# The values' bias inside the shared block product, a new order of a graph's operations, and the first weights on another DMA queue: a two-layer graph network on one Trainium2 core

## The chip, the cores and the metric

The kernel runs on one core of a Trainium2 chip. The metric is the device time of one launch, in microseconds. Engines are named as in the profile: PE is TensorE's matmul stream, PEld its weight loads, DVE is VectorE, ACT is ScalarE, POOL is GpSimd, SP is SyncE, which here only issues DMAs. A name with q, as SPq, is the engine's instruction queue.

## The reference

64 graphs of 256 nodes with 256 features go through two layers, all in float32. Cut to what matters:

```python
# layer 0, for each of 64 graphs: x (256, 256), adj (256, 256)
q = heads(x @ Wq + bq); k = heads(x @ Wk + bk)          # 8 heads of 32
attn = softmax(q @ k.T / sqrt(32))
for r in range(4):                                       # four relations
    v_r = heads(x @ Wv[r] + bv[r])
    out += (attn * (adj == r)) @ v_r
x = ln(x + out @ Wo + bo)
x = ln(x + gelu(x @ W1 + b1) @ W2 + b2)
# layer 1
h = gat(gat(x, adj, W1, a1), adj, W2, a2)                # masked softmax over nodes
h = ln(x + h)
x = ln(h + relu(h @ w_ff1 + b_ff1) @ w_ff2 + b_ff2)
```

## The kernel before, in words

A graph is one object, and its work is cut into 225 named operations, each a handful of instructions on one engine. The table PLACES gives each name a place on an axis. Graph g's operation stands at g * PERIOD + place, with PERIOD = 60, and all operations of all 64 graphs are sorted by that number and emitted in that order (`manual_schedule`, at the end of the kernel). So the places are no times: they set the order in which each engine meets its instructions, and how graphs are interleaved. An engine works its instructions strictly in that order and waits where an input isn't ready. Weight DMAs (L139, `issue_load`) and the one-time weight preparations (`v_weights`, `gat_weights`, two `ffn_weights`) stand in the same order at places of their own (LOAD_PLACE and LOAD_STEP, V_PLACE, FFA_PLACE, GAT_PLACE, FFB_PLACE). DMAs are issued on SP's queue.

The names, in the order in which a graph passes them (m is a half of the features, with four heads h each):

- load, cast, jT, mask0 to mask4: x and adj come in (L178, L180), adj is cast (L457), transposed by DMA (L462), and compared with 0 to 3 on GpSimd (L479); mask4 is the GAT mask (L471). xT and xS transpose x and form differences of its blocks (L446, L453).
- qk, qkc, s: query and key products (L487), copies out of PSUM on ScalarE (L496, L498), scores of four heads (L537), each with 32 rows of the array.
- max, exp, rec, nrm, eT, eW, eR: softmax on VectorE and ScalarE (L542 to L560), then a transpose through 32x32 squares on VectorE (L306) and a round trip through DRAM (L311 write, L315 read).
- ec copies the transposed weights to PSUM (L568), pm multiplies them with three relations' masks on VectorE (L572), pl with the fourth's on GpSimd (L577), po sums over relations and nodes (L589), each head in 32 columns of the array; oT copies it (L595).
- vp1 to vp7, vc1, va, vb: the values of all relations, by seven block products instead of eight (L511). vc1 copies the first product into block (0, 0) of v (L523, ScalarE), and the va operations (L520, VectorE) build the other blocks by adding products to blocks made before. vb1 and vb0 add the bias (L528, GpSimd).
- y, yb, wo, ya: residual and output product (L609, L613); st, rt, nb, ln: norms 1 to 4 (L347 to L364).
- aT, aW, aR, au, ax, aS, ad, ae: the first feed-forward part. Transposed input, up (L387), Gelu (L395), differences (L410), seven block products down (L422), sums (L430). The same letters with b: the second one, with Relu.
- hT to zdB, h10, h11, h2: the two GAT attentions (L619 to L682); store (L685).

PSUM has eight banks: four for the scores (s0 to s3), one po for the feed-forward sums, one pe for ec, and two, with the tag mm, that nearly all other products share. A product that takes one of the two waits until the last reader of the tile that lay there before is done. Of free banks, a product takes the one that was freed first in program order.

The two halves of the bias as before: block (m, jc) holds features of half m for node block jc, and the chain of the sums is

```python
for n, to, src, i in (("1", (0, 0), (0, 0), 2), ("6", (0, 1), (0, 0), 6), ("7", (1, 0), (0, 1), 7),
                      ("5", (1, 1), (1, 0), 5), ("4", (1, 0), (1, 0), 4), ("9", (0, 1), (0, 1), 5),
                      ("3", (0, 1), (0, 1), 3)):
    ops[f"va{n}"] = lambda to=to, src=src, i=i: self.v_sum(to, src, i)
```

Of the kernel before, what the change touches and what calls it, by code (L numbers as in the profile page):

```python
# [14 lines left out]
ALU = mybir.AluOpType  # L15
AX = mybir.AxisListType

P = 128
# [7 lines left out]

PERIOD = 60.0
PLACES = {
    "load": 51.115, "cast": 61.829, "xT": 85.66, "jT": 95.244, "mask0": 96.779, "qk0": 96.964,
    "qkc0": 97.949, "s0": 114.109, "mask1": 114.874, "max02": 120.516, "max01": 124.15, "exp02": 124.943,  # L30
    "rec02": 126.88, "nrm02": 128.516, "max00": 137.875, "max03": 138.248, "exp01": 142.049, "xS": 142.083,
    "eT02": 142.989, "exp00": 144.909, "rec01": 145.054, "qk1": 145.647, "exp03": 145.994, "eW02": 148.03,
    "rec00": 148.295, "qkc1": 149.435, "rec03": 149.477, "nrm01": 152.334, "mask2": 153.228, "vp1": 153.403,
    "nrm00": 154.4, "eT00": 155.05, "vc1": 155.594, "s1": 155.923, "nrm03": 158.066, "max10": 158.616,
    "max11": 159.127, "vp6": 159.308, "y": 159.875, "eR02": 161.643, "max13": 162.676, "mask3": 162.803,
    "exp10": 163.51, "exp13": 164.265, "va6": 164.378, "eW00": 164.574, "vp7": 165.766, "max12": 166.896,
    "vp2": 167.32, "eT03": 167.321, "exp12": 167.329, "va7": 168.263, "va1": 168.656, "pl02": 168.829,
    "eT01": 170.084, "vp5": 171.47, "vb1": 171.744, "va9": 173.956, "exp11": 174.017, "va5": 174.086,
    "eW01": 174.237, "vp4": 174.322, "rec11": 174.688, "rec10": 175.037, "ec02": 175.434, "nrm10": 175.847,
    "va4": 177.865, "nrm11": 178.881, "eW03": 179.53, "eT11": 180.637, "rec12": 181.004, "eR01": 181.498,  # L40
    "rec13": 182.146, "pm02": 182.221, "vp3": 182.341, "nrm13": 182.509, "eR00": 182.73, "mask4": 182.957,
    "ec01": 183.686, "va3": 183.974, "pl00": 184.596, "pm01": 184.674, "nrm12": 185.397, "eT13": 185.431,
    "eR03": 186.516, "ec00": 187.545, "eW11": 189.732, "eW13": 192.489, "pm00": 192.506, "eR11": 192.805,
    "pl03": 192.932, "pl01": 194.193, "ec03": 194.796, "vb0": 194.872, "pm03": 195.848, "eT10": 196.442,
    "eR13": 197.184, "eT12": 197.655, "po0": 199.032, "ec11": 199.429, "eW10": 200.338, "oT0": 203.052,
    "eW12": 203.488, "eR10": 203.542, "pm11": 203.833, "ec13": 205.99, "pm13": 207.559, "pl11": 208.544,
    "ec10": 209.569, "pm10": 210.783, "eR12": 211.055, "pl13": 211.531, "pl10": 212.738, "yb": 213.806,
    "ec12": 214.966, "pm12": 215.614, "pl12": 216.323, "po1": 224.021, "oT1": 226.193, "wo": 231.792,
    "ya": 235.114, "st1": 235.515, "rt1": 236.411, "nb1": 237.487, "ln1": 240.106, "aT": 241.237,
    "aW": 243.237, "aR": 244.635, "au0": 248.422, "au1": 248.889, "ax0": 249.225, "ax1": 250.028,  # L50
    "au2": 253.377, "aS1": 255.511, "ax2": 257.28, "au3": 257.297, "ag": 259.726, "ax3": 259.931,
    "ar": 263.256, "aS3": 265.084, "aS2": 265.188, "aS4": 266.76, "ad1": 267.736, "ad7": 268.061,
    "ad2": 269.978, "ad3": 270.34, "ad4": 270.945, "ae": 271.281, "ad5": 273.751, "ae1": 274.652,
    "ae7": 275.033, "ad6": 277.637, "ae5": 279.375, "ae6": 281.724, "st2": 283.997, "rt2": 284.29,
    "nb2": 285.905, "ln2": 291.498, "lg2": 293.887, "lb2": 294.79, "hT": 297.683, "hW": 300.513,
    "hR": 303.071, "ga0": 304.63, "gac0": 305.433, "ga1": 305.656, "gac1": 307.317, "ipA": 307.666,
    "zA": 307.902, "zmA": 307.921, "zxA": 308.379, "zeA": 312.657, "zdA": 315.675, "h10": 324.462,
    "h11": 325.343, "h1c0": 325.47, "h1c1": 325.478, "ipB": 327.18, "zB": 327.348, "zmB": 328.529,
    "zxB": 330.271, "zeB": 332.506, "zdB": 332.513, "h2": 335.643, "h2a": 335.996, "st3": 338.835,
    "rt3": 339.209, "nb3": 342.44, "ln3": 344.153, "bT": 344.795, "bW": 353.039, "bR": 353.733,  # L60
    "bu0": 358.326, "bu1": 358.559, "bx0": 358.988, "bu2": 361.425, "bx1": 361.898, "bx2": 361.904,
    "bu3": 362.148, "bx3": 363.223, "bS1": 363.277, "bd1": 364.353, "bg": 366.001, "bS2": 366.044,
    "br": 366.414, "bd5": 366.625, "bS4": 368.189, "bd6": 369.237, "bd2": 371.158, "bd3": 371.454,
    "be1": 372.63, "be5": 372.632, "bd4": 372.862, "bS3": 372.912, "be6": 374.175, "be": 375.364,
    "bd7": 377.598, "be7": 378.628, "st4": 383.514, "rt4": 389.43, "nb4": 404.438, "ln4": 418.122,
    "lg4": 419.704, "lb4": 422.082, "store": 423.961,
}
LOAD_PLACE, LOAD_STEP = 96.0, 3.0
V_PLACE, FFA_PLACE, GAT_PLACE, FFB_PLACE = 100.0, 240.0, 290.0, 300.0

# [11 lines left out]
def kernel(  # L84
# [12 lines left out]
    nc = tc.nc  # L97
    B, N, D = x.shape
    R = Wv.shape[0]
# [5 lines left out]
    C = N // P  # L105
# [28 lines left out]

    loads = []

    def issue_load():
        t, src = loads.pop(0)
        nc.sync.dma_start(t, src)  # L139

    def weight(w, name, mixed=False):

        k, n = w.shape[0] // P, w.shape[1]
        t = const.tile([P, k, n], F32, name=name)
        if mixed:
            mixed_rows(t, w)
        else:
            loads.append((t, w.rearrange("(k p) n -> p k n", p=P)))
        return t
# [13 lines left out]
    def rowvec(v, n, name):  # L163
        t = const.tile([P, n], F32, name=name)
        loads.append((t, _row(v, n)))
        return t
# [21 lines left out]
    bv_r = const.tile([P, KD, R, P], F32, name="bv_r")  # L188
# [4 lines left out]
        loads.append((bv_r[:, m],  # L193
                      bass.AP(tensor=bv.tensor, offset=bv.offset + m * P, ap=[[0, P], [D, R], [1, P]])))
    while loads:
        issue_load()
    wv_t = const.tile([P, 3, R * P], F32, name="wv_t")
    wv_s = {}
    scale = 1.0 / math.sqrt(DH)
# [4 lines left out]
    wo, bo_r = weight(Wo, "wo"), rowvec(bo, D, "bo_r")  # L204
# [44 lines left out]
    def seven_weights(b, t):  # L249


        nc.vector.tensor_tensor(t[0], b[0][1], b[1][1], ALU.add)
        nc.vector.tensor_tensor(t[1], t[0], b[0][0], ALU.subtract)
        nc.vector.tensor_tensor(t[2], b[1][0], t[1], ALU.subtract)
        nc.vector.tensor_tensor(b[0][1], b[0][0], b[0][1], ALU.subtract)
        return {1: b[0][0], 2: b[1][0], 3: t[2], 4: b[1][1], 5: t[0], 6: t[1], 7: b[0][1]}

    def v_weights():
        wv_s.update(seven_weights([[wv[:, k, m].rearrange("p r n -> p (r n)") for m in range(KD)] for k in range(KD)],
                                  [wv_t[:, i] for i in range(3)]))  # L260

# [170 lines left out]
    class Graph:  # L432
# [87 lines left out]
            nc.vector.tensor_tensor(self.v_part(*to), self.v_part(*src), self.ps["v", i], ALU.add)  # L520

        def v_first(self):
            nc.scalar.copy(self.v_part(0, 0), self.ps["v", 1])  # L523

        def v_bias(self, m, jcs):
            v = self.v[m][:, jcs]
            row = bv_r[:, m].rearrange("p r n -> p (r n)")[:, None, :]
            nc.gpsimd.tensor_tensor(v.rearrange("p c r n -> p c (r n)"), v.rearrange("p c r n -> p c (r n)"),  # L528
                                    row.to_broadcast([P, len(range(C)[jcs]), R * P]), ALU.add)

        def scores(self, m):

# [154 lines left out]
        def operations(self):  # L687

            g, ops = self.g, {}
# [8 lines left out]
            for i in range(1, 8):  # L698
                ops[f"vp{i}"] = lambda i=i: self.v_product(i)

            ops["vc1"] = self.v_first
            for n, to, src, i in (("1", (0, 0), (0, 0), 2), ("6", (0, 1), (0, 0), 6), ("7", (1, 0), (0, 1), 7),
                                  ("5", (1, 1), (1, 0), 5), ("4", (1, 0), (1, 0), 4), ("9", (0, 1), (0, 1), 5),
                                  ("3", (0, 1), (0, 1), 3)):
                ops[f"va{n}"] = lambda to=to, src=src, i=i: self.v_sum(to, src, i)
            ops["vb1"] = lambda: self.v_bias(1, slice(0, 1))
            ops["vb0"] = lambda: self.v_bias(0, slice(0, C))
            for r in range(R + 1):
                ops[f"mask{r}"] = lambda r=r: self.mask(r)
            for m in range(KD):  # L710
# [56 lines left out]


    plan = [(LOAD_PLACE + i * LOAD_STEP, len(PLACES), issue_load) for i in range(len(loads))]
    for place, f in (  # L770
            (V_PLACE, v_weights),
            (GAT_PLACE, gat_weights),
            (FFA_PLACE, lambda: ffn_weights(w1, b1_c, g1_c, be1_c, b2_r, be1_r, "ffa", w2, w2_t)),
            (FFB_PLACE, lambda: ffn_weights(f1, bf1_c, gl1_c, bl1_c, bf2_r, bl1_r, "ffb", f2, f2_t))):
        plan.append((place, len(PLACES), f))
    for g in range(B):
        ops = Graph(g).operations()
# [34 lines left out]
```

## Time and profile before

| what | us |
|---|---|
| median of three runs | 3575.66 (3571.31 to 3575.95) |
| the profiled execution, its own time | 3572.94 |
| its span, first to last instruction | 3571.2 |

The granted TensorE clock over the span is 0.985. The page of the profile gives each engine's busy time and share of the span. The chain of waits follows the instruction that ended last back to what released it, and back again, to the start. A timeline line is a run of equal instructions: start, length, engine, line, operation, output and inputs, shape, count, and in brackets the idle time before it with its releaser. A group's line gives busy time and the mean ns of one, then the engine's idle time before it.

### The profile page before, as it was taken

What the parts mean: (1) busy time and instruction counts of PE and PEld (TensorE: products, weight loads), DVE (VectorE), ACT (ScalarE), POOL (GpSimd) and SP (SyncE); (2) the same over time, 40 slices, a digit from 0 to 9 for tenths busy, and PEclk for the clock granted to TensorE, in tenths of its full rate; (3) what the DMA queues carried; (4) which work ended last, traced back from release to release, by engine and by line L of the source; (5) the groups of instructions that cost most, each with busy time, mean ns of one, the idle gap of its engine ahead of it and who ended that gap; (6) DMA issues with size and microseconds to landing.
All of it is one profiled execution on the core that took longest, in us unless ns stands there. A gap on an engine that the chain in (4) does not pass through costs nothing.

```text
span 3571.2 us, 73514 instructions
## 1 busy us (share of the span) xinstructions
PE 3477.1 (97%) x25816; PEld 2704.2 (76%) x25816; DVE 2805.2 (79%) x4952; ACT 2776.8 (78%) x7107; POOL 3117.9 (87%) x3398
## 2 busy tenths in 40 slices
PE   6899999999999999999999999999999999999995
PEld 3677877877877877877877877877877877877875
DVE  5788888888888888788788888888788788788762
ACT  4677877877877877877877877877877877877863
POOL 4688988988988988988988988988988988988974
PEclk8899999999999999999999999999999999999997
DMA  7344444444444444444444444444444444444420
GB/s 198 112 126 127 131 135 127 131 135 127 131 135 127 131 135 128 131 135 126 132 135 125 133 135 125 133 135 122 135 136 122 135 136 122 135 136 123 132 86 27
DMA packets 809890, 457.97 MB, mean 128 GB/s; under 512 B 334256, under 2 KB 718896, under 8 KB 809520
## 3 DMA queue, kind: packets, MB, share of 16 engines
q1 hardware_dynamic: 809520, 453.27, 43.2%
q8 instruction: 203, 3.33, 0.4%
q14 instruction: 167, 1.37, 0.1%
HBM read 243.42 MB, written 201.33 MB: 125 GB/s over the span
## 4 chain that ended last, share of the span: by engine, by line
PE 95%; DMA 1%; DVE 1%; SPq 1%; POOL 1%; ACT 0%; issue 0%; POOLq 0%; ACTq 0%; DVEq 0%
PE po L589 13%; PE ffa_ps L387 12%; PE ffb_ps L387 12%; PE v_ps L511 11%; PE qk_ps L487 6%; PE ffa_po L422 6%; PE ffb_po L422 6%; PE ffa_pq L422 5%; PE ffb_pq L422 5%; PE s L537 4%; PE h_ps L664 3%; PE h_ps L678 3%; PE ga_wps L619 3%; PE wo_ps L609 3%; SPq L139 1%; PE ga_ips L631 0%
## 5 line engine op out<-in xcount | busy, mean ns | idle before, releaser
L572 DVE TENSOR_TENSOR pm<-rel,pe 128x1536 f32<-128x1536 uint8 x512 | 890.9, 1740 | 131.9 <-ACT pe L568 85.3
L577 POOL TENSOR_TENSOR pl<-rell,eT 128x512 f32<-128x512 bf16 x512 | 592.1, 1168 | 29.0 <-DMA eT<-eT_d 24.2
L550 ACT ACTIVATE e<-s,nmax 128x256 f32<-128x256 f32 x1024 | 474.7, 471 | 73.2 <-DVE eT_sq L306 63.6
L387 PE MATMUL ffb_ps<-ffb_T,f 128*128 128x256 f32 x2048 | 458.4, 382 | 24.0 <-DMA ffb_T<-ffb_T_d 23.8
L387 PE MATMUL ffa_ps<-ffa_T,w 128*128 128x256 f32 x2048 | 465.9, 381 | 8.3 <-DMA ffa_T<-ffa_T_d 8.2
L387 PEld LDWEIGHTS ffb_ps<-ffb_T,f 128*128 128x128 f32 x2048 | 392.6, 192 | 106.1 <-issue 39.4
L560 ACT ACTIVATE e<-e,rden 128x256 f32<-128x256 f32 x1024 | 462.4, 506 | 10.3 <-DVE rden L555 10.1
L479 POOL TENSOR_SCALAR rel<-adT 128x512 uint8<-128x512 bf16 x192 | 288.6, 1503 | 198.1 <-DVE pm L572 181.1
L387 PEld LDWEIGHTS ffa_ps<-ffa_T,w 128*128 128x128 f32 x2048 | 381.3, 191 | 57.8 <-ACT e L560 9.6
L520 DVE TENSOR_TENSOR v<-v,v_ps 128x512 f32<-128x512 f32 x448 | 296.0, 672 | 148.2 <-PE v_ps L511 142.5
L589 PE MATMUL po<-pm,v 128*32 128x256 f32 x6144 | 361.6, 384 | 15.7 <-POOL v L528 12.3
L306 DVE STREAM_TRANSPOSE eT_sq<-e 128x512 f32<-128x512 f32 x512 | 350.6, 694 | 3.3 <-ACT e L560 1.9
L395 ACT ACTIVATE ffb_h<-ffb_ps,bf_c 128x256 f32<-128x256 f32 x512 | 214.6, 470 | 160.6 <-PE ffb_ps L387 154.7
L542 DVE TENSOR_REDUCE nmax<-s 128x2 f32<-128x512 f32 x512 | 337.0, 669 | 0.0
L589 PEld LDWEIGHTS po<-pm,v 128*32 128x32 f32 x6144 | 188.7, 110 | 184.1 <-ACT e L560 46.2
L568 ACT COPY pe<-eT 128x512 f32<-128x512 f32 x512 | 303.3, 592 | 17.8 <-DMA eT<-eT_d 12.7
L528 POOL TENSOR_TENSOR v<-v,bv_r 128x512 f32<-128x512 f32 (+1 forms) x128 | 232.9, 1819 | 5.4 <-DVE v L520 1.1
L395 ACT ACTIVATE ffa_h<-ffa_ps,b_c 128x256 f32<-128x256 f32 x512 | 208.5, 475 | 5.5 <-PE ffa_ps L387 3.8
L496 ACT ACTIVATE qT<-qk_ps,bqs_c 128x256 f32<-128x256 f32 x128 | 60.7, 474 | 188.5 <-PE qk_ps L487 188.5
L550 ACT ACTIVATION_READ_ACCUMULATOR e<-s,nmax 128x1 f32 x1024 | 205.8, 201 | 0.0
L354 POOL TENSOR_TENSOR rs_x<-rs_x,nhalf 128x2 f32<-128x2 f32 x256 | 184.0, 719 | 21.3
L430 DVE TENSOR_TENSOR ffa_res<-ffa_po,ffa_res 128x256 f32<-128x256 f32 (+2 forms) x256 | 133.4, 521 | 69.9 <-PE ffa_po L422 65.6
(154 smaller groups left out, 8535.9 us busy)
## 6 DMA issues: line engine op xcount, KB each, us to landing
eT_d<-eT_sq SPq DMA_DIRECT2D x512, 256.0 KB, 2.1
eT<-eT_d SPq DMA_DIRECT2D x512, 256.0 KB, 3.2
xin<-in_x_dram SPq DMA_DIRECT2D x256, 64.0 KB, 2.5
adi<-in_adj_dram SPq DMA_DIRECT2D x64, 256.0 KB, 3.2
y<-in_x_dram SPq DMA_DIRECT2D x64, 256.0 KB, 3.1
ffa_T_d<-ffa_T_sq SPq DMA_DIRECT2D x64, 256.0 KB, 2.6
ffa_T<-ffa_T_d SPq DMA_DIRECT2D x64, 256.0 KB, 2.9
hT_d<-hT_sq SPq DMA_DIRECT2D x64, 256.0 KB, 2.1
```

The source lines that it names most:

```text
L306: nc.vector.transpose(self.sq.rearrange("p a c k y -> p (c k) a y"), src.rearrange("p c (k a x) -> p (c k) a x", k=KD, a=A))
L387: nc.tensor.matmul(p[:, f - f0, :], self.wa[:, k, f * P:(f + 1) * P], self.x.nodes(k), start=(k == 0), stop=(k == KD - 1))
L395: nc.scalar.activation(self.h[half][:, f1 + f, :], self.ps[f0][:, f, :], self.func, bias=self.ba[:, f0 + f:f0 + f + 1])
L422: nc.tensor.matmul(self.p[bank][:, k], a[:, f], seven[self.name[:3]][i][:, f], start=(f == 0), stop=(f == KF // 2 - 1))
L511: nc.tensor.matmul(self.ps["v", i], a, wv_s[i], start=True, stop=True)
L542: nc.vector.tensor_reduce(self.nmax[m, h], self.s4[m][h].rearrange("p (c n) -> p c n", c=C), AX.X, ALU.max, negate=True)
L550: nc.scalar.activation(e[:, ic, :], self.s4[m][h][:, ic * N:(ic + 1) * N], AF.Exp, bias=self.nmax[m, h][:, ic:ic + 1], accum_out=self.den[ ...
L560: nc.scalar.activation(e[:, ic, :], e[:, ic, :], AF.Copy, scale=self.rden[m, h][:, ic:ic + 1])
L568: nc.scalar.copy(self.pe[m, h], self.et[m, h].t.rearrange("p b c k y -> p (b c k y)"))
L572: nc.vector.tensor_tensor(self.pm[m, h], self.rel.rearrange("p r b c k y -> p r (b c k y)"), bc(self.pe[m, h], [P, R - 1, C * N]), ALU.mult)
L577: nc.gpsimd.tensor_tensor(self.pm_l[m, h], self.rel_l.rearrange("p b c k y -> p (b c k y)"), self.et[m, h].t.rearrange("p b c k y -> p (b ...
L589: nc.tensor.matmul(po[hp, :], self.v[m][:, jc, r, hp], w, start=(r == 0 and jc == 0), stop=(r == R - 1 and jc == C - 1))
```

## The change

There are five edits.

1. The bias of half 0 is added where the first product leaves PSUM: vc1 becomes an add on VectorE instead of a copy on ScalarE. Since every other block is built from block (0, 0), the bias of half 0 reaches them all.
2. `v_weights` once replaces the bias row of half 1 by its difference to that of half 0, and vb1 adds that difference to block (1, 0) after va7, from which block (1, 1) is built. It stays on GpSimd with 512 columns. vb0, an add of 1024 columns, is left out.
3. All places are new. load stands at 98.4 instead of 51.1 and store at 490.8 instead of 424.0; the distances between stages, and so the neighbours on each engine, differ throughout. Taken by the remainder after division by 60, TensorE now has s1 directly before po0 (37.6 and 38.3), vp7, vp2, qk1, vp5, s0, vp3, wo in a row, all four of bu, and au0 to au3 near each other.
4. The places of the weight DMAs and preparations are new: LOAD_PLACE from 96 to 164.4, V_PLACE from 100 to 170, FFA_PLACE from 240 to 322, GAT_PLACE from 290 to 376, FFB_PLACE from 300 to 380.
5. The first ten weight DMAs (wq, wk, their biases, the values' weights and biases), which are issued before any planned operation, go to ScalarE's DMA queue; all later ones stay on SP's.

```diff
-LOAD_PLACE, LOAD_STEP = 96.0, 3.0
-V_PLACE, FFA_PLACE, GAT_PLACE, FFB_PLACE = 100.0, 240.0, 290.0, 300.0
+LOAD_PLACE, LOAD_STEP = 164.4, 3.0
+V_PLACE, FFA_PLACE, GAT_PLACE, FFB_PLACE = 170.0, 322.0, 376.0, 380.0
...
-    def issue_load():
+    def issue_load(engine=nc.sync):
         t, src = loads.pop(0)
-        nc.sync.dma_start(t, src)
+        engine.dma_start(t, src)
...
     while loads:
-        issue_load()
+        issue_load(nc.scalar)
...
+    def bias_row(m):
+        return bv_r[:, m].rearrange("p r n -> p (r n)")
+
     def v_weights():
+        nc.vector.tensor_tensor(bias_row(1), bias_row(1), bias_row(0), ALU.subtract)
         wv_s.update(seven_weights([[wv[:, k, m].rearrange("p r n -> p (r n)") for m in range(KD)] for k in range(KD)],
...
         def v_first(self):
-            nc.scalar.copy(self.v_part(0, 0), self.ps["v", 1])
-
-        def v_bias(self, m, jcs):
-            v = self.v[m][:, jcs]
-            row = bv_r[:, m].rearrange("p r n -> p (r n)")[:, None, :]
-            nc.gpsimd.tensor_tensor(v.rearrange("p c r n -> p c (r n)"), v.rearrange("p c r n -> p c (r n)"),
-                                    row.to_broadcast([P, len(range(C)[jcs]), R * P]), ALU.add)
+            nc.vector.tensor_tensor(self.v_part(0, 0), self.ps["v", 1], bias_row(0), ALU.add)
+
+        def v_bias(self):
+
+            nc.gpsimd.tensor_tensor(self.v_part(1, 0), self.v_part(1, 0), bias_row(1), ALU.add)
...
-            ops["vb1"] = lambda: self.v_bias(1, slice(0, 1))
-            ops["vb0"] = lambda: self.v_bias(0, slice(0, C))
+            ops["vb1"] = self.v_bias
```

The new order on TensorE over one period (the remainders of the places after division by 60, so neighbours belong to different graphs):

```
vp7 1.4  vp2 3.6  qk1 5.3  vp5 6.6  s0 8.7  vp3 9.0  wo 9.2
bu0 14.4 to bu3 16.6  vp4 18.1  bd1 20.5  ga0 20.6  ga1 22.1  bd5 23.7  ipA 24.1
bd2 24.8  bd6 25.0  bd3 27.1  bd4 28.0  au0 29.0  bd7 30.2  au1 31.4  au2 32.2  au3 34.8
s1 37.6  po0 38.3  h10 39.9  h11 41.6  vp1 42.6  ad1 42.8  ipB 43.2  ad6 43.5  qk0 44.6
ad7 45.6  vp6 46.7  ad5 50.3  ad2 50.7  h2 52.8  ad3 55.5  ad4 57.8  po1 59.1
```

## The prediction

> **What bounds the kernel now.** I read the page first, then the busy time by stretches, the chain of waits, TensorE's timeline of one graph, and the groups by shape.
>
> ```profile
> span 3571.2 us, 73514 instructions
> PE 3477.1 (97%) x25816; PEld 2704.2 (76%) x25816; DVE 2805.2 (79%) x4952; ACT 2776.8 (78%) x7107; POOL 3117.9 (87%) x3398
> ```
>
> The stretches (columns: stretch, its length, busy us and instructions of PE, PEld, DVE, ACT, POOL, then granted clock, DMA share, GB/s) say where TensorE is not full:
>
> ```profile
> 0.00:50.00 50.00, 26.20 (x86) 13.87 (x86) 21.37 (x41) 19.32 (x59) 17.81 (x23) 0.80 0.76 197
> 50.00:100.00 50.00, 33.35 (x246) 21.47 (x247) 38.00 (x56) 29.58 (x77) 29.42 (x29) 0.76 0.67 188
> 100.00:150.00 50.00, 45.22 (x332) 31.73 (x330) 35.88 (x61) 25.82 (x66) 32.93 (x35) 0.86 0.36 95
> 150.00:200.00 50.00, 45.52 (x319) 32.96 (x320) 38.28 (x66) 37.72 (x99) 34.55 (x39) 0.90 0.38 117
> 200.00:3400.00 3200.00, 3199.70 (x24006) 2499.45 (x24005) 2599.66 (x4585) 2586.27 (x6630) 2903.76 (x3156) 1.00 0.44 131
> 3400.00:3572.00 172.00, 127.11 (x833) 104.69 (x831) 72.01 (x146) 78.06 (x179) 99.44 (x119) 0.88 0.19 56
> ```
>
> From 200 to 3400 us TensorE is never idle and at full clock; the filling of the pipeline (0 to 200) leaves it idle for 50 us, the emptying (from 3400) for 45. The chain of waits gives the beat of the middle:
>
> ```profile
> 1001.33 6.91 PE ffb_ps L387 x32
> 1054.89 6.91 PE ffb_ps L387 x32
> ```
>
> One graph takes 53.56 us, some 61 times in all outside filling and emptying. Busy is not packed, though. In TensorE's timeline (start, length, ..., count), group starts show what a group really costs:
>
> ```profile
> 1023.17 1.05 PE L422 MATMUL ffb_po<-f,ffb_h 128*128 128x128 f32 x8
> 1024.16 2.80 PE L589 MATMUL po<-pm,v 128*32 128x256 f32 x48
> ...
> 1027.75 2.01 PE L664 MATMUL h_ps<-ga_wh,ga_z 128*128 128x258 f32 x8
> 1029.59 1.11 PE L487 MATMUL qk_ps<-xT,wq 128*128 128x256 f32 x4
> ...
> 1039.66 1.15 PE L537 MATMUL s<-kT,qT 32*128 32x256 f32 x16
> 1040.74 1.13 PE L487 MATMUL qk_ps<-xT,wq 128*128 128x256 f32 x4
> 1041.71 1.03 PE L487 MATMUL qk_ps<-xT,wk 128*128 128x256 f32 x4
> 1042.57 0.61 PE L422 MATMUL ffa_po<-w_t,ffa_t 128*128 128x128 f32 x4
> ```
>
> A full-array group of four 256-column matmuls takes 0.86 us (1041.71 to 1042.57). The one right after s takes 0.97, and s itself 1.08 where four rounds of 0.216 are 0.86. So a visit to the tiled forms (32*128 for s, 128*32 for po) costs: about 0.10 at entry (ffb_po 0.99 before po, 0.89 elsewhere), 0.13 to 0.22 at the exit, 0.10 in the first full group after it; 0.41 for s, 0.33 for po. There are four visits a graph.
>
> **What the Trainium skill says.** "TensorEngine Tiling (Array Packing)", Tiling Modes, Key Properties: changing the tiling mode drains the TensorE. The trace agrees (the 0.33 to 0.41 us above). "Trainium Kernel Development and Optimization", Key Constraints: DMAs of the SP and ACT queues run on the same 16 engines; another issuer saves only the sequencer's issue time. In the trace the engines are 0.76 busy in the first 50 us, so there is little spare rate. "ScalarE: Activation LUTs", What ACT_TABLE_LOAD costs: about 1283 ns plus a drain of about 1380. The trace agrees on 1283; the activation follows 10 to 20 ns later (1014.52 + 1.28, next start 1015.82), so I price a load at 1.28.
>
> **The change, part by part.**
>
> *Bias.* Removed per graph: GpSimd's vb0 and ScalarE's copy. Kept: a GpSimd add of 512 columns. Added: one VectorE add that replaces the copy, 672 ns by its row v<-v,v_ps.
>
> ```profile
> L528 POOL TENSOR_TENSOR v<-v,bv_r 128x1024 f32<-128x1024 f32 x64 | 151.4, 2366 | 0.0
> L520 DVE TENSOR_TENSOR v<-v,v_ps 128x512 f32<-128x512 f32 x448 | 296.0, 672 | 148.2 <-PE v_ps L511 142.5 <-POOL v L528 5.7
> L523 ACT COPY v<-v_ps 128x512 f32<-128x512 f32 x64 | 36.9, 577 | 0.0
> ```
>
> Per graph GpSimd falls by 2.37 us from 48.7 (3117.9/64), ScalarE by 0.58 from 43.4, VectorE rises by 0.67 from 43.8 to 44.5. All stay under TensorE's 53.56, so in the middle this alone is worth 0; the cover is TensorE's own work. The new wait: vc1 stands on VectorE between pm13 and pm11; behind it are pm11 and zmB (which the second GAT attention waits for), and TensorE's qk0 waits for the PSUM buffer that vc1 frees. From vp1's start to qk0 TensorE has 0.86 + 0.89 + 0.22 + 0.89 = 2.86 us (vp1, ad1, ipB, ad6); the product is complete about 1.02 after its start (second matmul at 0.43, 0.59 long), vc1 ends at 1.69. Spare: 1.2 us.
>
> *Places, in the middle.* I put TensorE's new order in a row with the durations above and walked the PSUM and buffer waits. New is that s1 stands directly before po0: three visits instead of four. The switch between the two tiled forms is not in the trace. Cheapest it costs nothing (0.41 saved), dearest as much as two separate visits (0). I take a drain like the others: 0.10 entry, 0.22 for the switch, 0.23 exit against 0.74 now: about -0.2. The 0.09 of the present qk1 after h10 (1029.59 to 1030.54 is 0.95) goes; vp5's wait of up to 0.19 for va7 passes to qk1, which now stands there. The other ties have 0.2 us or more to spare by ScalarE's starts: ipA after gac1, au2 after ax0, h10 after zdA, vp3 after qkc1. Together I take -0.25 us a graph, times 61 = -15 us; bounds -0.5 and +0.3, -30 to +18.
>
> ScalarE loses work too: ax0 to ax3 stand together with no exponential between, so two table loads a graph instead of four (by the groups of shapes now 127 at L395, 65 at L651, 62 at L550): -2.6 us a graph, off the path, but cover for those ties.
>
> *Filling.* The lines of the chain at the start:
>
> ```profile
> 4.20 0.47 SPq L139
> ...
> 54.69 2.31 POOL v L528
> 57.05 5.49 PE po L589 x64
> ...
> 90.37 2.02 DMA ffa_T_d<-ffa_T_sq
> 92.41 2.69 DMA ffa_T<-ffa_T_d
> 95.23 8.55 PE ffa_ps L387 x32
> ```
>
> SP's queue is the chain for most of the first 48 us. Ten weight DMAs leave it (4.20 to 10.0, 5.8 us); ScalarE issues them while idle (its first work is at 9.08), and if they lasted past that, qkc0 would pay. Bandwidth is shared, so xin may land up to 1 us later and the weights 1 to 2 us earlier. Given back: the next graph's four xin and one adi, 3.3 us, now stand before jT and another set before the first eR, and SP waits for the first transpose, some 3 us. Net on the first eR -1. The difference of the two bias rows is one more VectorE op at the head, +0.7, and waits for the last weight DMA. vb0 goes: 2.3 us straight off the chain before po. So po comes about 3 us earlier. Then aT now precedes the FFN weights' subtractions on VectorE (0.7 us each, four of them), whose time overlaps the 4.7 us of DMA: -3. Around the GAT weights (125 to 151 us) hT now comes before them: -4, bounds +6 and -12. Sum -10, bounds -20 and +6.
>
> *Emptying.* It is three rounds of ffb_ps, 40 to 44 us apart, each held by mask, softmax, norm and a DMA round trip. The lags of the stages behind wo differ by under 3 places (ffa 20 after 17, ffb 125 after 127, in places), so 0, bounds ±6.
>
> **Sum.** -15 - 10 = -25 us on the profiled 3572.9 us (span 3571.2 and 1.7 around it). The median of the runs is 3575.7, 2.7 higher; the same -25 gives 3550.
>
> **The rivals.**
> Both savings at their good ends (switch free, fill -20, so -30 - 20 = -50): 3525. For it speaks that all engines but TensorE get lighter on balance; against, that TensorE's order has many near ties. Chance 0.08.
> Nothing arrives: TensorE's 53.56 stays, the switch costs as much as the visit it saves, the weights are bandwidth bound and the fill gives back 5: 3571, range 3568.5 to 3583. Chance 0.13.
> Slower: VectorE serves vc1 late. If pm13 (1.74 us) starts later than 2.86 - 0.67 - 1.74 = 0.45 us after vp1's start, because its ec13 or eR13 is late, TensorE stands at qk0 in every graph; 1 us past that point is 61 us: 3550 + 61 = 3611, range 3583 to 3640. For it: the trace shows pm waiting for pe (85.3 us in 72 waits). Against: two fewer table loads make ec13 early. Chance 0.21.
>
> **The numbers.** Forecast, 3550 (own range 3530 to 3568): 0.58. A measurement tells about 0.2% from no change, 7 us. Faster 0.58 + 0.08 = 0.66, same 0.13, slower 0.21. The range 3518 to 3590 leaves out most of the slow case and a corner of the fast one, together under 0.2.
>
> **What would show it.** The beat between ffb_ps groups: 53.3. s directly before po, with the first h_ps late only once. Table loads about 128, POOL about 2966, DVE about 2850, ACT near 2580 us busy. vb0 gone and the first po near 54, the first ffa_ps near 89. I am wrong if TensorE shows gaps before qk0, ipA, au2 or h10 in every graph, if the beat is above 53.6, or if the first ffa_ps starts after 95.

## The result and the profile after

The changed kernel takes 3612.87 us (median of 4 runs, 3609.57 to 3614.64) beside 3575.14 us for the kernel before on the same chip (4 runs, 3571.31 to 3575.95). The ratio is 1.0104, 95% interval 1.0091 to 1.0117: slower by 1.0%, or 38 us, and outside the range of 3518 to 3590. The page after, the same two rows as before:

```profile
span 3609.6 us, 73073 instructions
PE 3487.7 (97%) x25816; PEld 2730.3 (76%) x25816; DVE 2856.3 (79%) x5017; ACT 2587.9 (72%) x6917; POOL 2986.9 (83%) x3334
```

Every total is within 1% of the forecast: VectorE 2856 (2850), ScalarE 2588 (2580), GpSimd 2987 (2966), and 129 table loads (128). The load of the engines was read rightly, and the time was not. The busy time by stretches (same columns as before):

```profile
...
100.00:150.00 50.00, 38.49 (x305) 27.88 (x304) 39.46 (x64) 30.95 (x79) 35.35 (x37) 0.90 0.42 120
...
200.00:3400.00 3200.00, 3184.58 (x23791) 2500.14 (x23790) 2627.71 (x4621) 2386.71 (x6398) 2763.18 (x3081) 1.00 0.45 130
```

TensorE now loses 15 us between 200 and 3400 us, where it lost none before, and does fewer matmuls in that time (23791 beside 24006). From 100 to 150 us it has 38 us of work rather than 45. The beat in the chain of waits:

```profile
1014.44 6.91 PE ffb_ps L391 x32
1068.35 6.91 PE ffb_ps L391 x32
```

The beat, the time from one graph's ffb_ps group to the next one's, is 53.91 us; before it was 53.56. With the start of the first ffb_ps group and of the 60th as marks, the two spans split without a rest:

| us | before | after | difference |
|---|---|---|---|
| filling, to the first ffb_ps | 197.7 | 204.5 | +6.8 |
| middle, 59 beats | 3161.6 | 3186.3 | +24.7 |
| emptying, from the 60th ffb_ps | 211.9 | 218.8 | +6.9 |
| span | 3571.2 | 3609.6 | +38.4 |

Of the middle's 24.7, 20.5 is the beat (0.347 times 59), and 4.2 is scattered beats that are 0.1 to 1 us longer (in those looked at, ffb_ps waits for its input's DMA).

**Two new waits in every graph.** A tie is a place where a group of TensorE needs something that another engine finishes. Two ties turned late. Around ipB (gb_ips) the timelines of TensorE, ScalarE and VectorE of the changed kernel read (start, length, what, and in brackets the idle time before and what ended it):

```profile
1044.86 1.05 PE L426 MATMUL ffa_po<-w,ffa_h 128*128 128x128 f32 x8
1046.11 0.43 PE L633 MATMUL gb_ips<-ident,gb_wh 128*128 128x128 f32 x2 [0.19 <-ACT gb_wh L672]
```

```profile
1043.33 0.38 ACT L672 COPY gb_wh<-h_ps 128x258 f32<-128x258 f32 x1 [0.59 <-PE h_ps L666]
1045.16 0.59 ACT L570 COPY pe<-eT 128x512 f32<-128x512 f32 x1 [1.45 <-DVE pm L574]
1045.69 0.37 ACT L672 COPY gb_wh<-h_ps 128x258 f32<-128x258 f32 x1
```

```profile
1043.35 1.74 DVE L574 TENSOR_TENSOR pm<-rel,pe 128x1536 f32<-128x1536 uint8 x1
1045.06 0.69 DVE L527 TENSOR_TENSOR v<-v_ps,bv_r 128x512 f32<-128x512 f32 x1
```

Read from below: pm13 reads the single PSUM bank pe until 1045.1. ec11 writes the same bank next, so ScalarE stands still for 1.45 us. h1c1, a copy whose input is complete near 1044.2, is queued behind ec11, and ipB needs h1c1. So ipB starts 1.25 us after the ffa_po group (ad1), where a packed group of that size, one followed at once by the next, takes 0.89. vc1, on which the slower rival was built, follows pm13 at once and is done at 1045.75; qk0 comes at 1047.27 and does not wait.

The second wait is at au1. TensorE's and VectorE's timelines:

```profile
1031.10 1.05 PE L426 MATMUL ffb_po<-f,ffb_h 128*128 128x128 f32 x8
1032.11 5.45 PE L391 MATMUL ffa_ps<-ffa_T,w 128*128 128x256 f32 x24
```

```profile
1027.84 0.42 DVE L434 TENSOR_TENSOR ffb_res<-ffb_po,ffb_res 128x256 f32<-128x256 f32 x1 [1.46 <-POOL ffb_t L414]
1030.09 0.78 DVE L644 COPY_PREDICATED_SCALAR ga_z<-no,negc 128x512 f32 x1
1030.91 0.69 DVE L648 TENSOR_REDUCE ga_max<-ga_z 128x2 f32<-128x512 f32 x1
1031.51 0.55 DVE L434 TENSOR_TENSOR ffb_res<-ffb_pq,ffb_res 128x384 f32<-128x384 f32 x1
```

be5 stands for 1.46 us (the profile names GpSimd's difference, which a product behind it needs), then the GAT's mask and maximum go ahead of be, the sum that frees the PSUM bank of ffb_pq. TensorE's next ffa_ps group (au1) takes that bank. It starts at 1032.11, as soon as be is done and 1.01 us after the ffb_po group before it, which packed takes 0.89.

### The profile page after: what moved, and what is told of

Same layout as the page of the kernel before. It is cut to its first block, busy times and chain, and to the rows that moved or that the text cites. A ratio compares the mean times of both kernels' runs of the same rounds, so it can differ in the third digit from the quotient of the medians.

```text
span 3609.6 us, 73073 instructions
## 1 busy us (share of the span) xinstructions
PE 3487.7 (97%) x25816; PEld 2730.3 (76%) x25816; DVE 2856.3 (79%) x5017; ACT 2587.9 (72%) x6917; POOL 2986.9 (83%) x3334
## 4 chain that ended last, share of the span: by engine, by line
PE 77%; DVE 10%; ACT 8%; DMA 3%; issue 1%; POOL 1%; SPq 1%; ACTq 0%; POOLq 0%; DVEq 0%
PE ffa_ps L391 12%; PE ffb_ps L391 12%; PE v_ps L515 9%; PE qk_ps L491 6%; PE ffb_po L426 6%; PE po L591 6%; PE ffa_po L426 5%; PE ffb_pq L426 4%; PE ffa_pq L426 4%; DVE pm L574 3%; DVE nmax L544 3%; PE ga_wps L621 3%; PE h_ps L680 3%; PE wo_ps L611 3%; ACT L653 2%; ACT ga_z L653 2%
## 5 line engine op out<-in xcount | busy, mean ns | idle before, releaser
L579 POOL TENSOR_TENSOR pl<-rell,eT 128x512 f32<-128x512 bf16 x512 | 590.3, 1170 | 193.3 <-DMA eT<-eT_d 102.5
L562 ACT ACTIVATE e<-e,rden 128x256 f32<-128x256 f32 x1024 | 455.1, 503 | 0.1
L434 DVE TENSOR_TENSOR ffb_res<-ffb_po,ffb_res 128x256 f32<-128x256 f32 (+2 forms) x256 | 129.2, 505 | 129.0 <-POOL ffb_t L414 104.2
L368 ACT ACTIVATE ffa_res<-ffa_res,nb_x,rs_x 128x256 f32<-128x256 f32 x256 | 140.1, 598 | 114.5 <-POOL nb_x L363 110.4
L357 POOL TENSOR_SCALAR rs_x<-mv_x 128x2 f32<-128x2 f32 x256 | 56.8, 222 | 154.7 <-DVE mv_x L353 119.4
```

Of the source, the lines that this page charges most:

```text
L562: nc.scalar.activation(e[:, ic, :], e[:, ic, :], AF.Copy, scale=self.rden[m, h][:, ic:ic + 1])
L579: nc.gpsimd.tensor_tensor(self.pm_l[m, h], self.rel_l.rearrange("p b c k y -> p (b c k y)"), self.et[m, h].t.rearrange("p b c k y -> p (b ...
```

## The experiments

Six of the eighteen kernels here keep parts of the kernel before, the others start from the changed one. The ratios are to runs of the kernel before on the same chip. Places are those of the table; 60 places are one beat.

**One part alone: the weights' queue.** In the kernel before, `issue_load(nc.scalar)` for the first ten weights:

> The kernel before with one edit: the ten initial weight DMAs are issued on ScalarE's queue. Theory (they now share the DMA engines with the first xin and delay it): first qk_ps near 12 us rather than 8, the first po 2 to 5 us later, beat unchanged, time +3 to +6 us (about 3578 to 3581). The step of the prediction (SP's queue is relieved): first po 1 to 6 us earlier, time -1 to -6. Rival (the fill is set by the places alone): within 2 us of before.

3577.06 us (3572.93 to 3580.22), ratio 1.0004 (0.9996 to 1.0012). First qk_ps at 10.8 instead of 8.0, first po 60.1 instead of 57.0, first ffb_ps 199.8 instead of 197.7, beat unchanged. And the other way round, `issue_load()` in the changed kernel:

> The changed kernel with the ten initial weight DMAs back on SP's queue. Theory (the shared engines delay the first xin): first qk_ps back near 8 us, first ffb_ps 3 to 6 us earlier than 204.5, time 3607 to 3610 where the changed kernel has 3613. Rival (the new places set the fill, the queue does not matter): first ffb_ps 203 to 206, time 3612 to 3614. Rival of the prediction (SP's queue is the bound and ScalarE's helps): slower, 3616 to 3619.

3611.35 us (3609.8 to 3611.63), ratio 1.0101 (1.0087 to 1.0114), first qk_ps back at 8.2, but first po at 65.6 (65.4 in the changed kernel) and first ffb_ps at 204.8. So the ten DMAs on ScalarE's queue do delay the first product by some 3 to 4 us. In the kernel before about 2 us of this are left at the first ffb_ps, and the time doesn't differ beyond its interval (-1.4 to +4.3 us); in the changed kernel nothing is left. The gain in the prediction falls, since the first po came later and not earlier, and my price of 3 to 6 us isn't seen either: the queue is worth nothing that can be measured, and does not explain the longer filling.

**One part alone: the bias.** The old places without vb0, with the code of the new bias and SP's loads:

```diff
-    "ec03": 194.796, "vb0": 194.872, "pm03": 195.848,
+    "ec03": 194.796, "pm03": 195.848,
```

> The kernel before, its places and its SP loads kept, with the new bias alone (vc1 an add on VectorE, vb1 adds the difference row, vb0 gone). Theory, as in the prediction: the middle does not feel it (beat 53.56), vb0's 2.3 us leave the fill: time 0 to -3 us. Rival (VectorE's extra 0.67 us makes pm or vc1 late in the middle): beat 53.6 to 54.0 and time +5 to +25 us, which would charge the loss of the whole change to the bias.

3587.28 us (3585.76 to 3590.18), ratio 1.0035 (1.0022 to 1.0048). The rival is right in its numbers: the bias is not free. What comes late is va7 and not pm or vc1. The chain of waits of this run shows the place; from 1041.1 to 1053.1 the chain is VectorE's alone, then it goes on with vp5 on TensorE:

```profile
1041.10 0.70 DVE ffa_res L434
...
1042.87 0.58 DVE v L527
1043.44 1.66 DVE pm L574
...
1052.53 0.58 DVE v L524
...
1053.16 1.12 PE v_ps L515 x2
```

The v at 1042.87 is vc1, new on VectorE; the v at 1052.53 is va7, for which TensorE waits at vp5. That wait existed before (0.19 us with its after-effect); counted from start to start against the packed product it grew from 0.09 to 0.28 us, and the beat from 53.565 to 53.756. Two tries to take it back by order: va7 from 168.263 to 166.0 (ahead of max12 and eT03), and then also max12 and eT03 to 168.7 and 168.8 and exp12 to 168.75 (behind va1).

> The kernel before with the new bias alone, as before_bias, and va7 placed directly behind bT on VectorE, ahead of max12 and eT03 (1.2 us of VectorE's queue). Theory (the 0.19 us a graph that the bias alone cost is TensorE's wait at vp5 for va7, which VectorE's extra add pushes later): beat 53.76 falls to 53.45 to 53.50, time 3587 - 16 = 3571. Rival (VectorE's queue as a whole has become the bound there): beat 53.6 to 53.76, time 3578 to 3587.

> The kernel before with the new bias alone, and max12, exp12 and eT03 placed behind va7 and va1 on VectorE (in the first try only va7 went ahead, and TensorE then stood at wo for va1). Theory (the 0.19 us that the bias alone costs is a matter of VectorE's order in front of vp5 and wo, with room left): beat 53.76 falls to 53.45 to 53.55, time 3568 to 3574. Rival (VectorE's load in that stretch is the bound, so that what is moved behind makes its own wait): beat 53.7 or above, time 3585 or more.

3667.65 us (1.0257, 1.0242 to 1.0273) and 3788.96 us (1.0602, 1.0587 to 1.0616), beats 54.99 and 57.07. In the first TensorE stands at wo for va1 instead (12.0 us of idle time in 18 graphs); in the second at s0, whose PSUM banks exp12 frees (27.2 us in 17 graphs). Both miss. So in these two orders each item that gives way (va1 in the first, max12 and exp12 in the second) is itself due for a step of TensorE. They fit the reading that VectorE's 0.67 us more in that stretch cost the 0.19, and don't prove it: other orders, and a version with load taken from VectorE elsewhere, were not tried.

**One part alone: the places.** The old bias needs a place for vb0, which the new table lacks. First 252.0, just behind va3; then 267.0, behind bS3.

> The kernel before, its bias and its SP loads kept, with the new places alone (vb0, which the new table lacks, put 0.4 places behind va3). Theory (the new order itself makes the waits at ipB, 0.40 us, and at au1, 0.23 us; the bias only adds to TensorE's wait for va7): beat 53.70 to 53.91, first ffb_ps near 206 to 208, time 3604 to 3614. Rival (without VectorE's extra add pm13 comes in time and the new order works as forecast): beat 53.3 to 53.5, time 3572 to 3590.

> The kernel before with the new places alone, as places_old_bias, but vb0 15 places later on GpSimd, behind bS3 and ahead of pl03, where po0 is still some 6 us away. Theory (the new order makes the waits at ipB and au1 by itself): beat 53.85 to 53.95, time 3608 to 3616. Rival (without VectorE's extra add the new order works as forecast): beat 53.3 to 53.5, time 3572 to 3590. If vb0 finds no room here either: beat above 54.2, time above 3630.

3774.62 us (1.0557, 1.0542 to 1.0571) and 3650.68 us (1.0210, 1.0196 to 1.0224). At 252.0 the 2.37 us on GpSimd stand ahead of the feed-forward differences, and TensorE waits for ffb_t. That measured my place for vb0, not the new order. At 267.0 this wait is gone, and the median beat is still 54.37 (54.1 to 56.5), as the last branch of the expectation has it. ipB's wait is there and longer (columns: busy us, mean ns, idle before; 19 graphs from 1000 to 2000 us):

```profile
L631 PE MATMUL gb_ips<-ident,gb_wh 128*128 128x128 f32 x38 | 8.2, 298 | 8.3 <-ACT gb_wh L670 8.3
```

ScalarE shows the same picture as in the changed kernel: h1c1 behind an ec11 that waits 1.50 us for pm13. au1's wait is there too, and of the same size: from the ffb_po group to au1 it is about 1.01 us in both runs, as in the changed kernel. So the new order makes both waits without the new bias. What is above the changed kernel's 53.91 is 0.24 us more at ipB and 0.22 at qk0, counted from start to start; in this run vc1, a copy on ScalarE again, stands behind h1c1 and ends at 1552.12, just before qk0 starts. With the old bias this order was slower at both places tried for vb0, so the two parts alone don't add up to the whole.

These two runs also place the longer filling and emptying. Their first ffb_ps comes at 205.5 and 210.2 us (197.7 before), and from the 60th ffb_ps on they take 220.6 and 221.2 us (211.9 before). They have the old bias and SP's loads, so the new places, those of the weight DMAs and preparations among them, are enough for both.

**The wait at ipB.**

```diff
-    "h1c1": 402.938,
+    "h1c1": 402.86,
```

That puts it ahead of ec11 (282.871, the same remainder 42.87 after division by 60) on ScalarE.

> The changed kernel with h1c1 placed just ahead of ec11 on ScalarE. Theory (TensorE stands 0.40 us at ipB in every graph because h1c1 is queued behind ec11, which waits for pm13): beat 53.91 falls to about 53.51, time 3613 - 24 = 3589. Rival (the delay only moves, to pm11 behind ec11 or to the next tie of TensorE): beat 53.75 to 53.91, time 3603 to 3613.

3586.45 us (3583.5 to 3589.5), ratio 1.0031 (1.0019 to 1.0042); beat 53.508, 0.404 less. As the theory said.

**The wait at au1.** be5 itself moves back by 1.8 places here, behind a transposition for the softmax and another graph's xT:

```diff
-    "zmA": 388.214, "zxA": 388.489, "be5": 445.136,
+    "zmA": 386.94, "zxA": 386.95, "be5": 446.96,
```

> The changed kernel with zmA and zxA (the first attention's mask and maximum) placed ahead of be5 on VectorE instead of behind be1. Theory (VectorE stands 1.46 us at be5 for GpSimd's ffb_t while the mask's input is ready, so be comes late and TensorE waits 0.23 us at au1; in the emptying the last graph's mask waits behind the be5 of the graph before): beat 53.91 falls to about 53.68, the last three beats of ffb_ps shrink by 5 to 7 us together, time 3613 - 14 - 6 = 3593. If pm13 also comes earlier, ipB's 0.40 us goes with it: beat 53.3, time 3570. Rival (the wait for be is set by TensorE's own bd4 or by the mask itself): beat within 0.05 of 53.91, time 3606 to 3614.

3596.59 us (3595.49 to 3599.0), ratio 1.0060 (1.0048 to 1.0073); beat 53.684, 0.228 less. The emptying hardly moves (217.8 us after 218.8): that half of the theory falls. Both edits together:

> The changed kernel with the two edits that each worked alone: h1c1 ahead of ec11, zmA and zxA ahead of be5. Theory (the waits at ipB and au1 are separate): beat 53.91 - 0.40 - 0.23 = 53.28, time 3613 - 26 - 16 = 3571. Rival (loosening both brings the wait at ffb_ps that the run with four ties showed): beat 53.45 to 53.75, time 3580 to 3600.

3573.51 us (3569.86 to 3575.3), ratio 0.9994 (0.9986 to 1.0002), 39 us under the changed kernel:

```profile
1003.92 6.91 PE ffb_ps L391 x32
1057.20 6.91 PE ffb_ps L391 x32
```

The beat is 53.28. The two waits add up (0.404 + 0.228 = 0.632; 53.912 - 53.278 = 0.634), and what remains is the beat of 53.3 that was forecast. The time is the kernel before's and not the 3550 forecast, since filling and emptying stay long (203.7 and 219.4 us).

**Four ties.** The same two, and va7 to 242.3 (ahead of bT), eR02 to 245.8 (behind the residual's load on SP):

> The changed kernel with four ties loosened by places alone: h1c1 ahead of ec11, zmA and zxA ahead of be5, va7 ahead of bT, and eR02 behind the residual's load on SP's queue (so that bW does not stand behind a read that waits for its write). Theory (the three waits of TensorE, 0.40 + 0.23 + 0.19 us a graph, are separate and add up, and what is left is packed but for the switches): beat 53.91 falls to about 53.10, the scattered longer beats go, middle 3186 to 3135, filling and emptying as in the changed kernel, time 3613 - 50 = 3563. Rival (one of the waits comes back elsewhere): beat 53.28 to 53.5, time 3572 to 3587.

3605.06 us (1.0081, 1.0065 to 1.0096). The waits came back at ffb_ps, for its DMA and for VectorE's steps; the beats vary from 53.4 to 56. In the run with two ties va7 waits for its own product (0.52 us), not for VectorE's queue, so putting it ahead made it wait longer there (1.12 us), with bT behind it.

**The tiled visits.** s1 from 217.552 to 214.6, between full-array groups again:

> The changed kernel with s1 moved from directly before po0 to directly before au3, between full-array groups: four visits to the tiled forms a graph again. Theory (a visit less saved 0.2 us a graph, as forecast): beat 53.91 + 0.2 = 54.11, time 3613 + 12 = 3625. Rival (what the switch between the two tiled forms costs is as much as a visit): beat within 0.05 of 53.91, time 3610 to 3616.

3681.78 us (1.0298, 1.0284 to 1.0312), beat 55.08. Neither theory: h10 now comes a microsecond earlier after the last ffa_ps group and waits for ScalarE's ga_wh (8.8 us of idle time in 18 graphs), ipB for vc1. s1 had been cover. The run doesn't price the switch; the starts of TensorE's matmuls in the changed kernel do:

```profile
1037.49 1.15 PE L539 MATMUL s<-kT,qT 32*128 32x256 f32 x16
1038.57 2.80 PE L591 MATMUL po<-pm,v 128*32 128x256 f32 x48
1041.18 1.05 PE L591 MATMUL po<-pl,v 128*32 128x256 f32 x16
1042.16 2.01 PE L666 MATMUL h_ps<-ga_wh,ga_z 128*128 128x258 f32 x8
```

A round is four tiled matmuls that start within 0.02 us of each other. Against packed matmuls, entering a tiled form costs 0.093 us, the second round within it 0.104 for s and 0.024 for po, leaving it 0.11, and the full-array group after it 0.104. From s directly to po there is the 0.11 of leaving s and po's 0.024, and neither the 0.104 nor a new 0.093. So the visit saved is worth 0.093 + 0.104 = 0.197 us.

**The filling.** load from 98.397 to 113.0 with cast at 113.2; and, on the run with two ties, load at 103.7 with cast at 115.0:

> The changed kernel with load and cast placed some 14 and 10 places later, so that the second graph's five input DMAs stand behind jT of the first graph, and the third graph's behind the first eR, as in the kernel before. Theory (these two sets ahead on SP's queue are why the filling got longer): the first eT write on SP's queue near 31 rather than 37 us, first po 59 to 62 rather than 65.4, first ffb_ps 198 to 202 rather than 204.5, beat unchanged, time 3607 to 3611. Rival (VectorE's order with the weights' sums holds the filling): first ffb_ps 203 to 206, time 3612 to 3614.

> The run with two ties, and load placed 5.3 places later (behind jT and the first eW on SP's queue) with cast 11 places behind it. Theory (the two input sets ahead on SP's queue lengthen the filling; the earlier try was spoilt by GpSimd's cast standing right behind its load): first po near 62, first ffb_ps 198 to 202, time 4 us under the run with two ties. Rival (the filling is set by the deeper order, not by SP): first ffb_ps 203 to 206, time within 2 us of the run with two ties.

3619.95 us (1.0128, 1.0114 to 1.0142) and 3574.36 us (0.9997, 0.9989 to 1.0005; 3573.51 without it). In the first, the first eT write came at 32.0 rather than 37.8 us, the first po at 62.9 and the first ffa_ps at 102.6 (106.7), about as expected, but the first ffb_ps at 209.8: GpSimd's cast stood right behind its own load, and the feed-forward differences behind the cast. In the second, without that fault, the first eT write came at 34.2 rather than 36.9 us, and nothing behind it did (first po 66.6, first ffb_ps 205.1). So the two input sets ahead on SP's queue are not what lengthens the filling. The weight DMAs at their new places, which fill most of SP's queue from 18 to 31 us, were not moved back alone. Single profiles scatter by some us here: in the changed kernel and its variants with load left in place the first ffb_ps lies between 200.9 and 206.5.

**The emptying.** For the last three graphs zeA at 393.3 (ahead of ax2) and zdA at 395.5; and, on the run with two ties, for the last graph alone zeA at 387.0 and zdA at 389.0. The edit of the second (the first has `g >= B - 3`):

```diff
-        plan += [(g * PERIOD + t, i, ops[n]) for i, (n, t) in enumerate(PLACES.items())]
+        places = {**PLACES, **LAST} if g == B - 1 else PLACES
+        plan += [(g * PERIOD + t, i, ops[n]) for i, (n, t) in enumerate(places.items())]
```

> The changed kernel with another place for two steps of the last three graphs alone: zeA (the first attention's exponential) ahead of ax2 and zdA ahead of be6. Theory (the longer emptying is made by the new order, in which that exponential stands behind all four gelu steps of the graph after, and its division behind the graph before's last sums): the last two beats of ffb_ps fall from 49.05 and 43.31 to about 45 and 41, middle as in the changed kernel, time 3613 - 6 = 3607. Rival (the rounds at the end are as long as their products and DMA trips, whatever the order): last beats within 1 us of 49.05 and 43.31, time 3611 to 3614.

> The run with two ties, and in the last graph alone zeA placed right behind zxA and zdA ahead of be. Theory (in the last round the first attention stands behind the last sums of the graph before it): the last beat of ffb_ps falls from about 43 to 39 or 40, time 3 to 4 us under the run with two ties. Rival (the round is as long as its own steps): last beat above 42, no difference in time.

3616.78 us (1.0114, 1.0099 to 1.0129): the last beats become 55.42, 51.12 and 40.89 where they were 48.03, 49.05 and 43.31, so the last falls and the ones before it rise by more. The same three graphs' edit on the run with four ties, from which 3557 was expected, gave 3608.23 us (1.0091, 1.0075 to 1.0108), with last beats of 55.63, 50.14 and 38.95: nothing gained there either. For the last graph alone 3568.81 us (3566.59 to 3571.62), ratio 0.9983 (0.9976 to 0.9990): its beat falls from 43.16 to 39.83, as expected.

**The scattered beats.** On that run, eR02 at 245.8:

> The run with two ties and the earlier steps of the last graph, and eR02 behind the residual's load on SP's queue. Theory (bW stands behind a read that waits for its own write, and a slow DMA there reaches TensorE at bu0; in the run with four ties it was va7 ahead of bT that hurt): beat 53.28, the excess of the scattered longer beats falls to about 1 us, time 0 to 4 us under 3569. Rival (it was the later read that hurt): beat 53.4 to 53.8, time 3575 to 3600.

3567.65 us (3562.53 to 3569.6), ratio 0.9978 (0.9969 to 0.9988). The middle doesn't answer (excess of the scattered beats 3.9 us, 1.9 without the edit), so that theory misses; the 1.2 us to the run without it lie within the two spreads. The beat stays at 53.28, so eR02 alone was not what hurt in the run with four ties. That leaves va7 ahead of bT, alone or together with eR02. These last two kernels are faster than both kernels of the change, and than the kernel before by 0.2%.

## Why the prediction was wrong, step by step

The forecast was 25 us less, and the profiled span grew by 38.4. Of these 63 us, 37 are the two new waits, 17 the filling (+6.8 instead of -10), 7 the emptying and 4 the scattered beats; the saving in the middle (0.29 us in each of 59 beats, where the forecast took 0.25 in 61) was 2 us larger than forecast.

- **The mode switch, -0.2 a graph:** right, 0.197. The prediction's 0.22 for the switch is s's second round (0.104) and the exit from s, so its sum of 0.55 for s and po together stands; the starts give 0.546. The 0.09 at qk1 after h10 went too, vp5's wait did pass to qk1, and the beat without the two new waits is 53.28 (53.3 forecast).
- **"The other ties ... have 0.2 us or more to spare by ScalarE's starts":** this step failed, and with it the sign. It lists ipA, au2, h10 and vp3, each by its producer's start in the old order, and in the changed kernel none of the four waits in every graph. The two that turned late, ipB after h1c1 and au1 after be, are not in the list. Both are copies or sums whose input is there in time and which stand in a queue behind another that waits. They cost 0.63 us a graph, 37 us in 59 beats, more than the saving of 0.29. The step's unfavourable bound (+0.3 a graph) was too near: the net is +0.35.
- **Bias worth 0 in the middle:** wrong in the old order, +0.19 us a graph in the run with the bias alone. The sum checked the spare time at qk0, and not vp5, whose wait for va7 was named in the same prediction. In the new order the bias can't be taken out without putting vb0 back, and at both places tried for it the kernel was slower, so there the bias has no price of its own.
- **The vc1 rival:** it priced 3611 and the kernel takes 3613, by coincidence. Its condition didn't come true: pm13 would have had to start later than 0.45 us after vp1, and it starts 0.65 us ahead of it (1043.35 and 1044.00). vc1 follows as soon as its product is complete, and TensorE doesn't stand at qk0. pm13 costs time all the same, by the PSUM bank that ec11 and, behind it, h1c1 wait for.
- **Filling -10:** +6.8. Terms that were right: vb0's 2.3 us leave the first po (57.0 to 54.7 in the run with the bias alone), from wo to ffa_ps it is 13.0 us after 17.7 (-3 forecast), and from there to ffb_ps 97.8 after 102.5 (-4 forecast). The last two are right in size; no run isolates their reasons. Terms that failed: the queue is worth nothing, vb0's 2.3 are hidden by the first ffb_ps (197.9 after 197.7), and the first po came at 65.4, not near 54. I looked at the lags behind wo only, and the loss lies ahead of it: the first wo comes 16 us later (93.7 after 77.5). There the new order is deeper: from qk0 to wo 144.5 places instead of 134.8, which in the middle are 127.0 us from qk0 to wo of one graph instead of 117.3. The new places are enough for the longer filling (205.5 and 210.2 with the old bias), and the weights' queue and the input sets on SP's queue are excluded. Whether it is this depth or the new places of the weight DMAs and preparations is not shown: the cause of the filling's 6.8 us stays open.
- **Emptying 0:** +6.9. The last three rounds before were 49.4, 44.3 and 39.3 us, not 40 to 44, and only the last two grew, by 4.8 and 4.0. Of it 3.3 is shown, on the run with two ties, to be the last graph's exponential and division behind steps of the graph before. The round before, 49.05 where it was 44.28, shows this chain in the changed kernel:

```profile
3507.73 5.20 PE ffa_ps L391 x24
...
3513.81 1.28 ACT L653
3515.10 1.10 ACT ga_z L653 x4
3516.23 0.18 DVE ga_rden L659
3516.43 0.52 ACT ga_wh L661
3516.99 3.81 PE h_ps L666 x8
```

The exponential stands behind all four Gelu steps, so the table loads saved (four to two a graph, counted as a gain of cover) may be paid here: some 4 us from the end of ffa_ps to h_ps, a table load of 1.28 among them. Moving it forward in three graphs lengthened other rounds, so this part is read from the chain and not shown by a run.

## What to carry to other kernels

In a hand-made order, walk every tie of the bounding engine, and for each producer ask not only when its input is ready but what stands ahead of it in its queue and what that waits for. A copy of 0.37 us behind a copy that waits for a PSUM bank cost 0.40 us a graph where one visit less to the tiled forms saved 0.20, and moving it by one position brought the 0.40 back. When stages are reordered, compare the lags of every stretch, also ahead of the middle. Here the whole depth from qk0 to store is the same (326.1 places after 327.0) while the stretch from qk0 to wo grew by 9.7, and the filling grew with it, though that this is the cause was not shown.

## What the runs showed of the hardware

The idle column understates a stall of TensorE. At ipB the profile shows 0.19 us of idle time, and removing the wait gained 0.404 a graph; at au1 it shows none, and removing it gained 0.228. The listed length of a group runs past the start of the next (s: 1.15 us listed, next start after 1.08), so it can cover a stall; the distance from start to start shows the loss: 1.25 and 1.01 us where 0.89 is packed, and the group that waited is slower by 0.05 and 0.104 once more. The 0.104 follows an exit from a tiled form and the waits at au1 and qk1 alike, and directly from s to po it doesn't. So a switch between the two tiled forms is cheaper than two visits by 0.197 us.
